# The short end of a perceiver layer: silu by tanh between gelus, a norm shared by two engines, a shorter scale chain, two output banks

## The chip, the core and the metric

The kernel runs on one core of one Trainium2 chip. The metric is the device time in microseconds. Before the change the median of three runs is 2131.52 us (2131.42 to 2131.52). Profiles name the engines PE (TensorE's products), PEld (its weight loads), DVE (VectorE), ACT (ScalarE), POOL (GpSimd) and SP (which issues most DMAs).

## The reference

One layer works on `x` (128 rows of 512) with a context of 12544 rows. Cut to what matters here:

```python
x = x + xattn(layernorm(x), ctx)             # 16 heads of 128, softmax over 12544 rows
x = x + lightning(layernorm(x))              # 16 heads of 32, silu(q), silu(k), silu(v), decay, gate, rms norm
x = x + ffn(layernorm(x))

def ffn(x):                                  # 512 -> 2048 -> 512
    h = gelu(silu(bitlinear158(x, w1, b1)))  # gelu by erf
    h = layer_norm(h, ln_g, ln_b)
    return bitlinear158(h, w2, b2)

def bitlinear158(x, w, b):
    x = x * rsqrt(mean(x * x) + 1e-5)
    scale = 127 / max(max(abs(x)), 1e-5)     # one per row
    xq = clip(round(x * scale), -128, 127) / scale
    return xq @ weight_quant(w).T + b        # weights -1, 0, 1 times their mean size
```

## The kernel before, in words

**The long part** takes the first 2040 us. Scores of the cross attention (L190) and their weighing of the context (L469) are formed on TensorE from operands split in a high and a low part. Jobs of later stages are laid beside the weighing: the weights of the feed-forward part are loaded, averaged, quantized and left in SBUF as BF16 (`w1q`, `w2q`), and `inverse` (L611) makes the reciprocals of their sizes.

**The short part** is a chain of small stages on one tile of 128 rows. `seq` keeps the instructions that it wraps in the order in which the program gives them; the rest is placed by the tile framework. Buffers of a pool are reused when the last reader is done. The stages, with their lines:

- `values` (L740) and `outs` (L761) end the cross attention, group by group. Weights for them and for the next stage come as 1 MB loads through SP's queue (helpers at L635 and L641), in the three buffers that `weight_tile` (L482) deals out in turn. Wk, Wq and Wv of the second attention are loaded during `outs(1)` to `outs(3)`, its Wo after the projections.
- `keep_warm` (L88) issues products of zeros, 128x512 in BF16, into a bank that nobody reads. They occupy TensorE where it would otherwise be idle.
- The second attention normalizes (L830 to L840), projects (`project_T`, L851; L875), forms the scores of 16 heads (`psc`, L889), multiplies by the decay (L901) and by the values (`po2`, L904: one product of 32 columns per head), gates and normalizes (L911 to L924), and projects onto `pp`, two banks of 256 columns (L930, L933).
- The feed-forward part normalizes `pp` to `xf`, finds the row's largest magnitude (L990), makes the scale `s` (`quant_scales`), raises by the constant MAGIC to round (`rounded`, L959 to L962), transposes (L968) and bounds (L973). The first product (`ph`, L1009) is taken out of PSUM with scale and bias in four quarters of 512 (L1010), ScalarE applies silu to each (L1011) and then gelu (L1013); VectorE gathers the statistics (L1014, L1024). Each quarter is then normalized in two steps, (h - mean) * g (L1030) and that times 1/deviation plus b (L1031); ScalarE squares it with a row sum (L1032), VectorE takes its largest magnitude (L1033). Row sum and maximum give the second scale, the quarters are rounded, transposed and multiplied by `w2q` into one bank `py` (L1048), and the result is scaled, added to `x2` and stored in two halves (L1064, L1065). `x2` holds attention output plus `b2` (L1001).
- 20 fillers of another kind (L1018) and 65 of `keep_warm` stand between the first product and the transposes of the second.

Of the kernel before, what the change touches and what calls it, by code (L numbers as in the profile page):

```python
# [16 lines left out]
P = 128  # L17
D = 512
# [15 lines left out]
def tile_perceiver_layer(  # L34
# [42 lines left out]
    left = const.tile([P, 24], F32, name="left")  # L77
# [531 lines left out]
    inv = const.tile([P, 2], F32, name="inv")  # L609

    def inverse():  # L611
        seq(nc.vector.tensor_scalar(m12, m12, 1.0 / (FF * D), EPS, ALU.mult, ALU.max))
        seq(nc.vector.reciprocal(inv, m12))
# [162 lines left out]
    wo[3] = by_rows(x_wo, 3)  # L776

# [16 lines left out]
    a_w = [by_cols(a_wk, 0)]  # L794
    outs(2)
    a_w.append(by_cols(a_wq, 0))
    outs(3)
    a_w.append(by_cols(a_wv, 0))
    wg1 = ctp.tile([P, NC, P], F32, tag="hi", name="wg1")
    nc.gpsimd.memset(wg1, 0.0)  # L800
    nc.sync.dma_start(out=wg1[:, :, :LHD], in_=a_wg1.rearrange("(c p) k -> p c k", p=P))
    wg2 = ctp.tile([P, D], F32, tag="hi", name="wg2")
    nc.gpsimd.memset(wg2, 0.0)
    nc.sync.dma_start(out=wg2[:LHD, :], in_=a_wg2)
    nwb = ctp.tile([P, 2, D], F32, tag="lo", name="nwb")
    nc.sync.dma_start(out=nwb[:, 0, :], in_=a_norm_w.partition_broadcast(P))
    nc.sync.dma_start(out=nwb[:, 1, :], in_=b2.partition_broadcast(P))
# [4 lines left out]
    zeros_r = work.tile([P, 512], F32R, name="zeros_r")  # L812
    nc.gpsimd.memset(zeros_r.bitcast(F32), 0.0)
    late = [keepp.tile([P, 8, 512], F32, name=f"uT{f}") for f in range(2)]
# [49 lines left out]
    seq(nc.scalar.activation(qT, project_T(a_w[1]), AF.Silu))  # L864
    seq(nc.scalar.activation(kT, project_T(a_w[0]), AF.Silu))
    a_w.append(by_rows(a_wo, 0))
# [7 lines left out]
    for cc in range(NC):  # L874
        seq(nc.tensor.matmul(pv, lhsT=xaT[:, cc, :], rhs=a_w[2][:, cc, :], start=(cc == 0), stop=(cc == NC - 1)))  # L875
# [23 lines left out]
    for r in range(4):  # L899
        sc = late[1][:, 4 + r, :].rearrange("p (e q) -> p e q", e=NC)  # L900
        seq(nc.vector.tensor_tensor(sc, pscs[r], decayed[:, r, :, :], ALU.mult))  # L901
        for e in range(NC):
            cs = slice((4 * e + r) * LHD, (4 * e + r + 1) * LHD)
            seq(nc.tensor.matmul(po2[:, cs], lhsT=sc[:, e, :], rhs=v[:, cs], start=True, stop=True))  # L904
# [22 lines left out]
    for i in range(NC):  # L927
        for half, hs in enumerate(halves):
            if i < 2:
                seq(nc.tensor.matmul(pp[half], lhsT=ogT[:, i, :], rhs=a_w[3][:, i, hs], start=False, stop=False))  # L930
    for half, hs in enumerate(halves):
        for i in (2, 3):
            seq(nc.tensor.matmul(pp[half], lhsT=ogT[:, i, :], rhs=a_w[3][:, i, hs], start=False, stop=(i == 3)))  # L933
    keep_warm(ps_w, 14)
# [3 lines left out]
    def quant_scales(am, rms):  # L938


        floor = col("floor")
        seq(nc.vector.tensor_scalar(floor, rms, EPS, None, ALU.mult))
        step_ = col("step")
        s = col("s")
        seq(nc.vector.tensor_scalar(step_, am, floor, 1.0 / 127.0, ALU.max, ALU.mult))
# [10 lines left out]
    def rounded(dst, y, s, engine):  # L956

        if engine is nc.scalar:
            seq(nc.scalar.activation(y, y, AF.Identity, scale=s, bias=magic))  # L959
        else:  # L960
            seq(nc.vector.tensor_scalar(y, y, s, MAGIC, ALU.mult, ALU.add))
        seq(nc.vector.tensor_scalar(dst, y, -MAGIC, 127.0, ALU.add, ALU.min))  # L962
# [19 lines left out]
    less = col("less")  # L982
    seq(nc.vector.tensor_scalar(less, mv1[:, 0:1], -1.0, None, ALU.mult))
    rms1 = col("rms")
    seq(nc.scalar.activation(rms1, mv1[:, 1:2], AF.Sqrt, scale=1.0 + EPS, bias=eps2))
    xf = work.tile([P, D], F32, tag="xa", name="xf")
    seq(nc.scalar.activation(xf[:, halves[1]], pp[1], AF.Identity, bias=less))
    seq(nc.vector.tensor_scalar(xf[:, halves[0]], pp[0], mv1[:, 0:1], None, ALU.subtract))
    am1 = col("am")
    seq(nc.vector.tensor_reduce(am1, xf, AX.X, ALU.max, apply_absolute_value=True))  # L990
    s1, step1 = quant_scales(am1, rms1)
# [125 lines left out]
```

## Time and profile before

| | |
|---|---|
| median of three runs | 2131.52 us |
| profiled execution | 2134.19 us, its span 2132.5 us |
| long part ends | 2040.6 us |
| loads for the projections of the second attention | Wk at 2061.8, Wq at 2065.3, Wv at 2068.7, Wo at 2079.6 us |
| first product of the feed-forward part starts | 2103.6 us |
| scale `s` of its second product ready | 2122.6 us |
| the two stores are issued | 2129.4 and 2129.8 us |
| ScalarE's table loads from 2062 us on | six, 1.28 us each |

In a line of the chain or timeline, start and length come first, then engine, line and tiles; "x8" counts instructions. A float32 product appears as two records. A line of groups gives count, busy time, mean length of one, and the idle time of the engine ahead of it with what ended it. PEclk is TensorE's granted clock as a share of full speed.

### The profile page before, as it was taken

What the parts mean: (1) busy time and instruction counts of PE and PEld (TensorE: products, weight loads), DVE (VectorE), ACT (ScalarE), POOL (GpSimd) and SP (SyncE); (2) the same over time, 40 slices, a digit from 0 to 9 for tenths busy, and PEclk for the clock granted to TensorE, in tenths of its full rate; (3) what the DMA queues carried; (4) which work ended last, traced back from release to release, by engine and by line L of the source; (5) the groups of instructions that cost most, each with busy time, mean ns of one, the idle gap of its engine ahead of it and who ended that gap; (6) DMA issues with size and microseconds to landing.
All of it is one profiled execution on the core that took longest, in us unless ns stands there. A gap on an engine that the chain in (4) does not pass through costs nothing.

```text
span 2132.5 us, 23984 instructions
## 1 busy us (share of the span) xinstructions
PE 2120.1 (99%) x9627; PEld 1748.0 (82%) x9627; DVE 1647.5 (77%) x1825; ACT 753.9 (35%) x844; POOL 26.1 (1%) x16
## 2 busy tenths in 40 slices
PE   8999999999999999999999999999999999999999
PEld 7888888888888888888888888888888888888885
DVE  6877777777777777778897888887787777777735
ACT  6221222212222122214444444444444444444424
POOL 0000000000000000000000000000010000000010
PEclk9999999999999999999999999999999999999999
DMA  5333333333333333346564555454444444444360
GB/s 195 146 138 128 148 135 142 138 128 148 135 142 138 129 148 136 141 158 216 210 235 158 178 178 178 173 199 144 145 141 147 148 148 148 148 145 139 133 209 25
DMA packets 70766, 326.22 MB, mean 153 GB/s; under 512 B 7264, under 2 KB 11616, under 8 KB 45184
## 3 DMA queue, kind: packets, MB, share of 16 engines
q1 hardware_dynamic: 70512, 324.57, 42.0%
q8 instruction: 75, 1.23, 0.2%
q14 instruction: 35, 0.29, 0.0%
q10 hardware_dynamic: 144, 0.13, 0.0%
HBM read 221.65 MB, written 103.02 MB: 152 GB/s over the span
## 4 chain that ended last, share of the span: by engine, by line
PE 98%; DMA 1%; DVE 0%; ACT 0%; issue 0%; SPq 0%; DVEq 0%; ACTq 0%
PE pu L469 50%; PE ps L190 44%; PE pw L92 1%; PE pc L740 1%; DMA kq<-in_x_wq_dram 1%; PE po L761 0%; PE pk L364 0%; PE pp L851 0%; DMA wq<-in_x_wq_dram 0%; DMA kq<-in_a_wq_dram 0%; PE pq L344 0%; PE po L904 0%; PE py L1048 0%; PE pv L875 0%; PE pw L1018 0%; PE pp L930 0%
## 5 line engine op out<-in xcount | busy, mean ns | idle before, releaser
L190 PE MATMUL ps<-kq,cth 128*128 128x512 f32 x2744 | 844.5, 389 | 0.0
L469 PE MATMUL pu<-ph,cl 128*128 128x512 f32 x1568 | 610.0, 389 | 0.0
L469 PE MATMUL pu<-pl,ch 128*128 128x512 f32 x1568 | 610.0, 389 | 0.0
L469 PE MATMUL pu<-ph,ch 128*128 128x512 f32 x1568 | 610.0, 389 | 0.0
L190 PEld LDWEIGHTS ps<-kq,cth 128*128 128x128 f32 x2744 | 515.0, 188 | 106.8
L190 PE MATMUL ps<-kq,ctl 128*128 128x512 f32 x1344 | 522.8, 389 | 0.0
L523 ACT CAST ph<-si 128x1024 fp32r<-128x1024 f32 x194 | 203.9, 1051 | 491.3 <-PE pu L469 491.2
L469 PEld LDWEIGHTS pu<-pl,ch 128*128 128x128 f32 x1568 | 294.3, 188 | 61.3
L469 PEld LDWEIGHTS pu<-ph,cl 128*128 128x128 f32 x1568 | 294.3, 188 | 61.0
L469 PEld LDWEIGHTS pu<-ph,ch 128*128 128x128 f32 x1568 | 294.3, 188 | 61.0
L219 DVE TENSOR_TENSOR so<-ps,u 128x512 f32<-128x512 f32 x294 | 202.9, 690 | 134.8 <-PE ps L190 130.4
L190 PEld LDWEIGHTS ps<-kq,ctl 128*128 128x128 f32 x1344 | 252.3, 188 | 52.5
L511 DVE TENSOR_TENSOR cl<-cr,ch 128x1024 fp32r<-128x1024 f32 x98 | 120.2, 1227 | 204.7 <-ACT ch L505 204.7
L254 ACT COPY so<-ps 128x512 f32<-128x512 f32 x98 | 57.7, 589 | 577.5 <-PE ps L190 577.5
L528 DVE TENSOR_TENSOR pl<-si,ph 128x1024 fp32r<-128x1024 f32 x194 | 242.5, 1250 | 1.0 <-ACT ph L523 1.0
L237 DVE TENSOR_TENSOR mx<-mx,so 128x1024 f32<-128x1024 f32 x190 | 232.3, 1223 | 6.7
L517 DVE TENSOR_TENSOR si<-si,mb 128x1024 f32<-128x1024 f32 x194 | 235.7, 1215 | 0.0
L536 DVE TENSOR_TENSOR lsum<-lsum,si 128x1024 f32<-128x1024 f32 x192 | 233.9, 1218 | 0.0
L518 ACT ACTIVATE si<-si 128x1024 f32<-128x1024 f32 x194 | 205.5, 1059 | 61.0 <-DVE si L517 61.0
L505 ACT CAST ch<-cr 128x1024 fp32r<-128x1024 f32 x98 | 102.3, 1044 | 0.3 <-DMA cr<-in_c_dram 0.3
L176 DVE TENSOR_TENSOR ctl<-ctr,cth 128x1792 fp32r<-128x1792 f32 x47 | 94.9, 2019 | 0.7 <-ACT cth L171 0.7
L171 ACT CAST cth<-ctr 128x1792 fp32r<-128x1792 f32 x48 | 81.7, 1703 | 37.5 <-PE ps L190 35.4
(210 smaller groups left out, 769.2 us busy)
## 6 DMA issues: line engine op xcount, KB each, us to landing
sc<-so SPq DMA_DIRECT2D x98, 1024.0 KB, 3.8
si<-sc SPq DMA_DIRECT2D x97, 1024.0 KB, 4.9
cr<-in_c_dram SPq DMA_DIRECT2D x98, 512.0 KB, 3.4
ctr<-in_cT_dram SPq DMA_DIRECT2D x48, 512.0 KB, 3.5
kq<-in_w1T_dram SPq DMA_DIRECT2D x16, 512.0 KB, 4.6
kq<-in_w2T_dram SPq DMA_DIRECT2D x16, 512.0 KB, 4.8
kq<-in_x_wv_dram SPq DMA_DIRECT2D x3, 1024.0 KB, 5.4
kq<-in_x_wo_dram SPq DMA_DIRECT2D x3, 1024.0 KB, 7.4
```

The costliest lines, as they stand in the source:

```text
L176: return lo, nc.vector.tensor_tensor(lo, raw[:, :7, :, :], hi, ALU.subtract)
L190: nc.tensor.matmul(ps, lhsT=lt[:, a, cc, :], rhs=right(f, b, part)[:, cc, :], start=(first and n == 0), stop=(n == 5), skip_group_check=True,)
L219: place(nc.vector.tensor_tensor(to, t[p], t[q], ALU.add))
L237: place(nc.vector.tensor_tensor(mx[f], mx[f], t["so"][:, j, :], ALU.max))
L469: nc.tensor.matmul(pu[b][cc], lhsT=lt[:, j, cs], rhs=rt[:, bs], start=(first and n == 0), stop=(last and n == 2))
L505: seq(nc.scalar.copy(ctx_hi[f, i], ctx_raw[f, i]))
L511: seq(nc.vector.tensor_tensor(ctx_lo[f, i], ctx_raw[f, i], ctx_hi[f, i], ALU.subtract))
L517: seq(nc.vector.tensor_tensor(exps[k], exps[k], mb[f], ALU.subtract))
L518: seq(nc.scalar.activation(exps[k], exps[k], AF.Exp))
L523: seq(nc.scalar.copy(high[k], exps[k]))
L528: seq(nc.vector.tensor_tensor(low[k], exps[k], high[k], ALU.subtract))
L536: seq(nc.vector.tensor_tensor(lsum[f], lsum[f], exps[k], ALU.add))
```

## The change

- Wq of the second attention is loaded into the upper half of the first context sum's buffer (`uT0`, free after `values(1)`), ahead of `wo[3]`; Wk, Wv and Wo follow in the three dealt buffers. The small loads and memsets stand earlier in the program.
- The `po2` products of head r of four are 128, 96, 64 and 32 columns wide: each writes also the columns of later heads, which the later products overwrite.
- The floor under a scale is a constant and no longer EPS times the row's size; the maxima are joined in pieces, the sign of `xf` is turned (and of `s`), the sums of squares are used only for `dq2`.
- The additions into `x2` follow the four L1010. Quarters 0 and 1 keep silu on ScalarE; for quarters 2 and 3, ScalarE gives tanh(h/2), VectorE (tanh + 1) * h, and gelu takes half of it. Gelus, tanhs, multiplications and statistics are interleaved in a written order.
- In the last norm, quarter 0 stays on VectorE. For quarters 1 to 3 TensorE adds identity times b and diagonal(1/deviation) times (h - mean) g in PSUM, where squares, maxima and rounding read them.
- The second rounding raises all quarters first, begins with a half quarter, and its product goes into two banks of 256 columns. Filler counts change: 14 to 13 ahead of the first rounding, 20 + 65 to 12 + 14 behind it.

```diff
+    inv = const.tile([P, 3], F32, name="inv")
+    m1_neg = inv[:, 2:3]
     def inverse():
         seq(nc.vector.tensor_scalar(m12, m12, 1.0 / (FF * D), EPS, ALU.mult, ALU.max))
-        seq(nc.vector.reciprocal(inv, m12))
+        seq(nc.vector.reciprocal(inv[:, :2], m12))
+        seq(nc.vector.tensor_scalar(m1_neg, m12[:, 0:1], -1.0, None, ALU.mult))
...
     outs(0)
     wo[3] = by_rows(x_wo, 3)
+    late = [keepp.tile([P, 8, 512], F32, name="uT0")]
+    a_w = {"q": by_cols(a_wq, 0, lambda shape: late[0][:, 4:, :])}
...
     outs(1)
     values(3)
-    a_w = [by_cols(a_wk, 0)]
+    late.append(keepp.tile([P, 8, 512], F32, name="uT1"))
+    a_w["k"] = by_cols(a_wk, 0)
     outs(2)
-    a_w.append(by_cols(a_wq, 0))
+    a_w["v"] = by_cols(a_wv, 0)
     outs(3)
-    a_w.append(by_cols(a_wv, 0))
...
-    zeros_r = work.tile([P, 512], F32R, name="zeros_r")
-    nc.gpsimd.memset(zeros_r.bitcast(F32), 0.0)
-    late = [keepp.tile([P, 8, 512], F32, name=f"uT{f}") for f in range(2)]
     keep_warm(ps_w, 8)
...
         seq(nc.vector.tensor_tensor(sc, pscs[r], decayed[:, r, :, :], ALU.mult))
         for e in range(NC):
-            cs = slice((4 * e + r) * LHD, (4 * e + r + 1) * LHD)
+            cs = slice((4 * e + r) * LHD, (4 * e + 4) * LHD)
             seq(nc.tensor.matmul(po2[:, cs], lhsT=sc[:, e, :], rhs=v[:, cs], start=True, stop=True))
...
-    keep_warm(ps_w, 14)
+    keep_warm(ps_w, 13)
     x2 = late[1][:, 4, :]
-    def quant_scales(am, rms):
-        floor = col("floor")
-        seq(nc.vector.tensor_scalar(floor, rms, EPS, None, ALU.mult))
+    def quant_scales(am, others, sign):
         step_ = col("step")
         s = col("s")
-        seq(nc.vector.tensor_scalar(step_, am, floor, 1.0 / 127.0, ALU.max, ALU.mult))
+        seq(nc.vector.tensor_scalar(step_, am, others, sign / 127.0, ALU.max, ALU.mult))
         seq(nc.vector.reciprocal(s, step_))
         return s, step_
...
-    def rounded(dst, y, s, engine):
+    def raised(t, y, s, engine):
         if engine is nc.scalar:
-            seq(nc.scalar.activation(y, y, AF.Identity, scale=s, bias=magic))
+            seq(nc.scalar.activation(t, y, AF.Identity, scale=s, bias=magic))
         else:
-            seq(nc.vector.tensor_scalar(y, y, s, MAGIC, ALU.mult, ALU.add))
-        seq(nc.vector.tensor_scalar(dst, y, -MAGIC, 127.0, ALU.add, ALU.min))
+            seq(nc.vector.tensor_scalar(t, y, s, MAGIC, ALU.mult, ALU.add))
+    def rounded(dst, t):
+        seq(nc.vector.tensor_scalar(dst, t, -MAGIC, 127.0, ALU.add, ALU.min))
...
         seq(nc.vector.bn_stats(out=st1[:, half, :], in_=pp[half]))
     mv1 = small.tile([P, 2], F32, tag="mv", name="mv1")
     seq(nc.vector.bn_aggr(out=mv1, in_=st1))
-    less = col("less")
-    seq(nc.vector.tensor_scalar(less, mv1[:, 0:1], -1.0, None, ALU.mult))
+    xf = work.tile([P, D], F32, tag="xa", name="xf")
+    am1 = small.tile([P, 2], F32, tag="am1", name="am1", bufs=1)
+    seq(nc.scalar.activation(xf[:, halves[1]], pp[1], AF.Identity, scale=-1.0, bias=mv1[:, 0:1]))
+    seq(nc.vector.tensor_scalar(xf[:, halves[0]], pp[0], -1.0, mv1[:, 0:1], ALU.mult, ALU.add))
     rms1 = col("rms")
     seq(nc.scalar.activation(rms1, mv1[:, 1:2], AF.Sqrt, scale=1.0 + EPS, bias=eps2))
-    xf = work.tile([P, D], F32, tag="xa", name="xf")
-    seq(nc.scalar.activation(xf[:, halves[1]], pp[1], AF.Identity, bias=less))
-    seq(nc.vector.tensor_scalar(xf[:, halves[0]], pp[0], mv1[:, 0:1], None, ALU.subtract))
-    am1 = col("am")
-    seq(nc.vector.tensor_reduce(am1, xf, AX.X, ALU.max, apply_absolute_value=True))
-    s1, step1 = quant_scales(am1, rms1)
+    seq(nc.vector.tensor_reduce(am1[:, 0:1], xf[:, halves[0]], AX.X, ALU.max, apply_absolute_value=True))
+    seq(nc.vector.tensor_scalar(am1[:, 0:1], am1[:, 0:1], EPS * EPS, None, ALU.max))
+    seq(nc.vector.tensor_reduce(am1[:, 1:2], xf[:, halves[1]], AX.X, ALU.max, apply_absolute_value=True))
+    s1, step1 = quant_scales(am1[:, 1:2], am1[:, 0:1], -1.0)
     xq = work.tile([P, D], BF16, tag="g1T", name="xq")
     xqT = work.tile([P, NC, P], BF16, tag="xqT", name="xqT")
-    rounded(xq[:, halves[0]], xf[:, halves[0]], s1, nc.vector)
-    rounded(xq[:, halves[1]], xf[:, halves[1]], s1, nc.scalar)
+    for hs, engine in zip(halves, (nc.vector, nc.scalar)):
+        raised(xf[:, hs], xf[:, hs], s1, engine)
+        rounded(xq[:, hs], xf[:, hs])
     ptx = [transposed_b(xq[:, hs]) for hs in halves]
     for half in range(2):
         bounded(xqT[:, 2 * half : 2 * half + 2, :], ptx[half])
-    dq1 = taken_back(step1, rms1, m12[:, 0:1])
-    for half, hs in enumerate(halves):
-        seq(nc.vector.tensor_tensor(x2[:, hs], pp[half], nwb[:, 1, hs], ALU.add))
+    dq1 = taken_back(step1, rms1, m1_neg)
     hb = late[0][:, 4:, :].rearrange("p a b -> p (a b)")
     st = small.tile([P, 4, 6], F32, tag="bn4", name="st", bufs=1)
     fss = [slice(f * 512, (f + 1) * 512) for f in range(4)]
-    for fs in fss:
+    for f, fs in enumerate(fss):
         ph = ps_m.tile([P, 512], F32, tag="m", name="ph")
         for cc in range(NC):
             nc.tensor.matmul(ph, lhsT=xqT[:, cc, :], rhs=w1q[cc // 2][:, cc % 2, fs], start=(cc == 0), stop=(cc == NC - 1))
-        nc.vector.scalar_tensor_tensor(hb[:, fs], ph, dq1, rows["b1"][:, fs], ALU.mult, ALU.add)
-        seq(nc.scalar.activation(hb[:, fs], hb[:, fs], AF.Silu))
-    for f, fs in enumerate(fss):
-        seq(nc.scalar.activation(hb[:, fs], hb[:, fs], AF.Gelu))
-        nc.vector.bn_stats(out=st[:, f, :], in_=hb[:, fs])
...
...
-    keep_warm(ps_w, 65)
+        seq(nc.vector.scalar_tensor_tensor(hb[:, fs], ph, dq1, rows["b1"][:, fs], ALU.mult, ALU.add))
+        if f < 2:
+            seq(nc.scalar.activation(hb[:, fs], hb[:, fs], AF.Silu))
+    curve = late[1][:, 6:, :]
+    def bent(f):
+        seq(nc.scalar.activation(curve[:, f - 2, :], hb[:, fss[f]], AF.Tanh, scale=0.5))
+    def gelu(f):
+        seq(nc.scalar.activation(hb[:, fss[f]], hb[:, fss[f]], AF.Gelu, scale=1.0 if f < 2 else 0.5))
+    def times(f):
+        seq(nc.vector.scalar_tensor_tensor(hb[:, fss[f]], curve[:, f - 2, :], 1.0, hb[:, fss[f]], ALU.add, ALU.mult))
+    def spread(f):
+        seq(nc.vector.bn_stats(out=st[:, f, :], in_=hb[:, fss[f]]))
+    for half, hs in enumerate(halves):
+        seq(nc.vector.tensor_tensor(x2[:, hs], pp[half], nwb[:, 1, hs], ALU.add))
+    for do, f in (
+        (gelu, 0), (bent, 2), (spread, 0), (gelu, 1), (times, 2), (bent, 3), (spread, 1), (gelu, 2), (times, 3),
+        (spread, 2), (gelu, 3), (spread, 3),
+    ):
+        do(f)
     mv = small.tile([P, 2], F32, tag="mv", name="mv")
-    nc.vector.bn_aggr(out=mv, in_=st)
-    rh = row_rsqrt(mv[:, 1:2])
+    seq(nc.vector.bn_aggr(out=mv, in_=st))
+    pn = {}
+    for f, (pool, tag) in zip((1, 2, 3), ((ps_s, "s"), (ps_m, "m"), (ps_m, "m"))):
+        pn[f] = pool.tile([P, 512], F32, tag=tag, name="pn")
+        seq(nc.tensor.matmul(pn[f], lhsT=ident, rhs=rows["lb"][:, fss[f]], start=True, stop=False))
+    keep_warm(ps_w, 12)
+    rh = col("rh")
+    seq(nc.scalar.activation(rh, mv[:, 1:2], AF.Sqrt, bias=eps_t))
+    diagonal = work.tile([P, P], F32, tag="g1T", name="diagonal")
     sm4 = small.tile([P, 4], F32, tag="sm4", name="sm4", bufs=1)
-    am4 = small.tile([P, 4], F32, tag="am4", name="am4", bufs=1)
+    am5 = small.tile([P, 5], F32, tag="am5", name="am5", bufs=1)
+    seq(nc.vector.memset(am5[:, 0:1], EPS * EPS**0.5))
     junk = late[1][:, 5, :]
     for f, fs in enumerate(fss):
-        nc.vector.scalar_tensor_tensor(hb[:, fs], hb[:, fs], mv[:, 0:1], rows["lg"][:, fs], ALU.subtract, ALU.mult)
-        nc.vector.scalar_tensor_tensor(hb[:, fs], hb[:, fs], rh, rows["lb"][:, fs], ALU.mult, ALU.add)
-        nc.scalar.activation(junk, hb[:, fs], AF.Square, accum_out=sm4[:, f : f + 1])
-        nc.vector.tensor_reduce(am4[:, f : f + 1], hb[:, fs], AX.X, ALU.max, apply_absolute_value=True)
-    sm2, am2 = col("sm"), col("am")
+        seq(nc.vector.scalar_tensor_tensor(hb[:, fs], hb[:, fs], mv[:, 0:1], rows["lg"][:, fs], ALU.subtract, ALU.mult))
+        if f == 0:
+            seq(nc.vector.reciprocal(rh, rh))
+            seq(nc.scalar.mul(diagonal, ident, rh))
+        else:
+            seq(nc.tensor.matmul(pn[f], lhsT=diagonal, rhs=hb[:, fs], start=False, stop=True))
+    seq(nc.vector.scalar_tensor_tensor(hb[:, fss[0]], hb[:, fss[0]], rh, rows["lb"][:, fss[0]], ALU.mult, ALU.add))
+    whole = {**pn, 0: hb[:, fss[0]]}
+    for f in (1, 0, 2, 3):
+        seq(nc.scalar.activation(junk, whole[f], AF.Square, accum_out=sm4[:, f : f + 1]))
+    others = col("others")
+    for f in range(4):
+        if f == 3:
+            seq(nc.vector.tensor_reduce(others, am5[:, 0:4], AX.X, ALU.max))
+        seq(nc.vector.tensor_reduce(am5[:, f + 1 : f + 2], whole[f], AX.X, ALU.max, apply_absolute_value=True))
+    keep_warm(ps_w, 14)
+    s2, step2 = quant_scales(am5[:, 4:5], others, 1.0)
+    hq = work.tile([P, FF], BF16, tag="hq", name="hq")
+    py = [ps_v.tile([P, 256], F32, tag="v", name="py") for _ in range(2)]
+    hT = [work.tile([P, NC, P], BF16, tag="hT", name="hT", bufs=2) for _ in range(4)]
+    def outward(ns, halves_):
+        for n in ns:
+            for half in halves_:
+                seq(
+                    nc.tensor.matmul(
+                        py[half], lhsT=hT[n // 4][:, n % 4, :], rhs=w2q[n // 8][:, n % 8, halves[half]],
+                        start=(n == 0), stop=(n == NF - 1),
+                    )
+                )
+    raised(hb[:, halves[0]], hb[:, halves[0]], s2, nc.vector)
+    raised(hb[:, halves[1]], hb[:, halves[1]], s2, nc.scalar)
+    for f in (1, 2, 3):
+        raised(hb[:, fss[f]], pn[f], s2, nc.scalar)
+    pts = {}
+    for half in range(2):
+        rounded(hq[:, halves[half]], hb[:, halves[half]])
+        pts[half] = transposed_b(hq[:, halves[half]])
+    bounded(hT[0][:, 0:2, :], pts[0])
+    outward((0, 1), range(2))
+    rounded(hq[:, fss[1]], hb[:, fss[1]])
+    bounded(hT[0][:, 2:4, :], pts[1])
+    pts[1] = transposed_b(hq[:, fss[1]])
+    outward((2, 3), range(2))
+    for f in (2, 3):
+        rounded(hq[:, fss[f]], hb[:, fss[f]])
+        bounded(hT[f - 1], pts[f - 1])
+        pts[f] = transposed_b(hq[:, fss[f]])
+        outward(range(4 * f - 4, 4 * f), range(2))
+    bounded(hT[3], pts[3])
+    sm2, rms2 = col("sm"), col("rms")
     seq(nc.vector.tensor_reduce(sm2, sm4, AX.X, ALU.add))
-    seq(nc.vector.tensor_reduce(am2, am4, AX.X, ALU.max))
-    rms2 = col("rms")
     seq(nc.scalar.activation(rms2, sm2, AF.Sqrt, scale=1.0 / FF, bias=eps_t))
-    s2, step2 = quant_scales(am2, rms2)
-    hq = work.tile([P, FF], BF16, tag="hq", name="hq")
-    py = ps_v.tile([P, D], F32, tag="v", name="py")
-    hT = [work.tile([P, NC, P], BF16, tag="hT", name="hT", bufs=2) for _ in range(4)]
-    def outward(f):
-        bounded(hT[f], pts[f])
-        for n in range(4 * f, 4 * f + 4):
-            seq(
-                nc.tensor.matmul(
-                    py, lhsT=hT[f][:, n % 4, :], rhs=w2q[n // 8][:, n % 8, :], start=(n == 0), stop=(n == NF - 1)
-                )
-            )
-    pts = []
-    for f, fs in enumerate(fss):
-        rounded(hq[:, fs], hb[:, fs], s2, nc.scalar if f else nc.vector)
-        pts.append(transposed_b(hq[:, fs]))
-        if f > 0:
-            outward(f - 1)
     dq2 = taken_back(step2, rms2, m12[:, 1:2])
-    outward(3)
+    outward(range(12, 16), (0,))
+    outward(range(12, 16), (1,))
     y = work.tile([P, D], F32, tag="xa", name="y")
-    for half in range(2):
-        hs = slice(half * 256, (half + 1) * 256)
-        seq(nc.vector.scalar_tensor_tensor(y[:, hs], py[:, hs], dq2, x2[:, hs], ALU.mult, ALU.add))
+    for half, hs in enumerate(halves):
+        seq(nc.vector.scalar_tensor_tensor(y[:, hs], py[half], dq2, x2[:, hs], ALU.mult, ALU.add))
         (nc.sync, nc.scalar)[half].dma_start(out=out[:, hs], in_=y[:, hs])
     keep.close()
     att.close()
```

## The prediction

> **What bounds the kernel now.** I read the page's busy times and chain first, then the chain in order of time over the last 70 us, then groups, clock and single engines there. Page:
>
> ```profile
> PE 2120.1 (99%) x9627; PEld 1748.0 (82%) x9627; DVE 1647.5 (77%) x1825; ACT 753.9 (35%) x844; POOL 26.1 (1%) x16
> PE 98%; DMA 1%; DVE 0%; ACT 0%; issue 0%; SPq 0%; DVEq 0%; ACTq 0%
> ```
>
> TensorE is the bound, but the diff touches nothing of the two products (L190, L469) that fill it until 2040.6 us. What it touches lies behind, where the 98% mislead: much of TensorE's work there is filler on zeros (`pw`). The chain in order of time (start, us, what):
>
> ```profile
> 2065.28 6.73 DMA kq<-in_a_wq_dram
> ...
> 2087.15 3.73 PE po L904 x32
> 2090.87 4.25 PE pw L92 x13
> ...
> 2107.48 2.30 PE pw L1018 x20
> 2109.82 14.19 PE pw L92 x65
> 2124.01 0.24 PE ptb L968 x4
> ```
>
> Three things are to be seen: the projections wait for the load of Wq; 13 fillers take 4.25 us, 0.327 each, where 65 take 0.218 each; and the last fillers end at 2124.01, later than the `hq` that the transposes need. The clock explains the second (stretch, length, TensorE busy, granted clock, DMA share, GB/s):
>
> ```profile
> 2083.42:2086.84 3.42, 3.41 (x40) 1.00 0.25 95
> 2086.84:2090.25 3.41, 3.41 (x32) 1.00 0.00 0
> 2090.25:2093.66 3.41, 3.41 (x12) 0.50 0.00 0
> ```
>
> The stretch at half clock follows 3.1 us of `po2` products only 32 columns wide. They come 0.115 us apart like 128-column ones, so I estimate that each streams a quarter of that. Under the other fillers (L1018, L92 x65) the true chain runs on ScalarE and VectorE (groups since 2062; count, then busy, mean ns, idle before):
>
> ```profile
> L1010 DVE SCALAR_TENSOR_TENSOR uT<-ph,dq,row_b 128x512 f32<-128x512 f32 x4 | 3.0, 748 | 0.5 <-PE ph L1009 0.4
> L1031 DVE SCALAR_TENSOR_TENSOR uT<-uT,rsr,row_lb 128x512 f32<-128x512 f32 x4 | 2.8, 746 | 0.0
> L1033 DVE TENSOR_REDUCE am<-uT 128x1 f32<-128x512 f32 x4 | 2.5, 678 | 0.0
> L1014 DVE BATCH_NORM_STATS2 st<-uT 128x6 f32<-128x512 f32 x4 | 2.5, 681 | 2.6 <-ACT uT L1013 2.6
> L1013 ACT ACTIVATE uT<-uT 128x512 f32<-128x512 f32 x4 | 2.2, 618 | 0.0
> L1013 ACT ACT_TABLE_LOAD x1 | 1.3, 1283 | 0.0
> L959 ACT ACTIVATE uT<-uT,right,s 128x512 f32<-128x512 f32 x3 | 2.2, 803 | 0.7 <-DVE s L946 0.7
> L875 PE MATMUL pv<-kq,xaT 128*128 128x512 f32 x8 | 3.6, 592 | 0.0
> ```
>
> In the timeline, successive operations of one engine start about 0.08 us before the other ends when they are independent. A result is seen by another engine 0.03 to 0.05 us later, and a matmul's 0.17 us after its stream.
>
> **The change part by part**, in times of before.
>
> *Load of Wq.* It moves ahead of `wo[3]` in SP's queue, to about 2048.2, into `uT0`, which is free once `values(1)` is done. The product (L851) then waits only for ScalarE's copy `xaT`, which ends at 2071.74, so it starts at 2071.80 and not 2072.14: **0.34 us**. Behind Wq stand `wo[3]`, two rows, Wk, Wv, Wo; the queue moves some 310 GB/s there, so one more MB delays each by 3.4 us. `wo[3]` lands near 2062 (needed 2065.3), Wk near 2072.5 (needed 2075.4), Wv near 2075.5 (needed 2079.8), all covered; Wk 3 us later still would stall TensorE by what exceeds its cover. The POOL memsets and the mask move too: `df` now stands behind four reciprocals, so `decay` is complete near 2060 and is needed at 2085.9. Nothing.
>
> *Wider `po2`.* Widths 128, 96, 64, 32 at the same 0.115 us cost nothing, as L740's 128 columns at 0.112 show. I estimate the window's streaming at 2.06 of 3.41 us, 60%, against 30% before; the window 2069.77 to 2073.18, some 59% by the same count, kept its clock. So the 13 fillers take 2.8 us and end at 2093.3. The transposes then wait for VectorE (L924, first half done near 2093.4) and the copy for L930 ends 0.9 us later: L930 starts at 2094.35 in place of 2095.80. Beyond the 0.34 that is **1.1 us**. If the clock still falls it is nothing.
>
> *First scale.* `less` and `floor` go, the maximum is taken in halves (410 + 150 + 410 ns against 690 + 140): `s` comes 0.05 us sooner. The reciprocal sign and `m1_neg` are free, the latter within the long loop.
>
> *First product's way out.* The two additions into `x2` (0.61 us) move behind the four L1010. The first now starts when `ph` is done, 2104.52 for 2104.80; the second ends at 2106.12. Two silu instead of four follow, so the Gelu table is loaded from 2106.80 to 2108.08, where before it began at 2108.95: 2.15 us. Two tanh (618 ns, as L1013; built without a table load between) and two multiplications (748) come in. VectorE is now what orders it: after gelu 0 at 2108.72 it runs statistics, multiplication, statistics, multiplication, starting 0.60 to 0.67 apart, to 2111.36; the last gelu ends at 2112.00, its statistics at 2112.71, the aggregate at 2113.00 (was 2113.69). ScalarE's root is seen at 2113.61 (was 2114.04).
>
> *Norm shared.* VectorE keeps four L1030 and one L1031 instead of four; three are replaced by an identity and a diagonal product each, 0.86 us apiece (two records of 0.43, as L875). Identity products and 12 fillers end by 2112.4 under the gelus. The four L1030 and the reciprocal run to 2115.87, L1031 to 2116.53; diagonal products are done at 2115.63, 2116.50, 2117.35. Squares take 720 ns with their accumulator: 2116.38, then the one on the SBUF quarter 2117.28, 2118.03, 2118.78. In the built program each maximum over a PSUM bank waits for the square of that bank. The Trainium skill (PSUM — Partial Sum Buffer, Terms) says why: two engines on one bank at once collide, reads against reads included. The row is before's L1033, which read the same SBUF quarter while L1032 squared it. By the row `s` would be 0.3 us sooner; I take the rule, as the waits are in the program. So the third maximum starts at 2118.05, the fourth at 2118.85, and `s`, with 0.1 us for doubled waits, is ready at 2120.05 (was 2122.57): 2.5 us.
>
> *Rounding and output.* Roots and row sums leave the scale's chain. From `s` to the second `y` before: 7.18 us. Now the first transposes wait for a half (350 + 290 ns), not for fillers that overran by 0.45; ScalarE's 600 + 3 x 711 ns, then the last transposes, 0.42 us of bounding and eight 256-column products of 0.11 follow, and the first `y` runs beside the second bank's products. Followed through, that is 6.55 us: 0.65 less. The late `dq2` is ready within 0.05 us of the first bank. With 0.05 and 2.5, this is **3.15** after rounding.
>
> Sum: 0.34 + 1.1 + 3.15 = 4.6. The profiled execution took 2134.19 (span 2132.5) and would take 2129.6; the runs' median 2131.52 lies 2.67 below it, and I carry the difference over: **2126.9**.
>
> *What may take back a part.* Between the 12 fillers and the first diagonal product TensorE is idle for 2.2 us (2112.4 to 2114.6); before, fillers stood there. The row above says that 30% streaming in a 3.41 us window, without any idling, cost the clock in the next. If one window holds all of the gap, it streams 35%. The skill (TensorE: Matmul & The Clock Gate, Why this matters for your kernels) says that idle gaps must not exceed some 3 us. By the rule 2126.9 stands. By the row two diagonal products take 0.86 more each and the next 14 fillers, which otherwise end 0.4 us before the transposes, end 1.0 after their due time: 2127.9. The threshold is between 30 and 59%, the window must lie just so and the gap be as long as I work out; narrowly I take no loss. Both ends stay in the range.
>
> **The rivals.** (1) *Half clock for one window*, 2127.9: for it, 35% is near 30%; before's low stage and its end (2131.21, twelve times 3.413 later) put a window at 2110.73 to 2114.14, where the gap would fall; against it, the rule. (2) *The wider products don't save the clock*: 2128.0 with, 2129.0 together with (1). Against it the 59% window. (3) *Slower than before*: the clock stays at half from the diagonal products to the end. Two products, 14 fillers and all output work gain 9.1 us of TensorE time, 8.2 of it on the chain: 2135.1. It decides from about the fourth low window on (three cost 4.2, under the 4.6 gained). Against it, a TensorE kept busy at half clock got its clock back at 2093.66. (4) *More is gained*: PSUM reads on ScalarE shorter than SBUF ones (L880's 597 against L1011's 630) and fewer waits than I count: 2125.8.
>
> **How the numbers follow.** Main case 0.50 (own range 2126.1 to 2127.7), (1) 0.33, (2) 0.06, (3) 0.05, (4) 0.06. Low 2125.7 and high 2128.9 leave out (3), half of (2) and little of the tails. About 0.2%, 4.3 us, is what a measurement of this kernel can tell from no change: the bound is 2127.26. The main case passes it by 0.36: three quarters of its chance, 0.39, with 0.06 of (4) and 0.05 of (1), are faster: 0.50. Slower by over 0.2% is only the worse part of (3): 0.04. The rest, 0.46, is within.
>
> **What would show it.** L930's counterpart 1.4 us sooner with clock 1.00 ahead of it; the Gelu table load 2.1 us sooner against the chain; `s` 2.5 us sooner after the attention's last product; no filler ahead of the last transposes in the chain. Clock 0.50 behind the gap, with 14 fillers of 0.22 us each reaching into the transposes, shows (1). Wrong would be the sum if a load is waited for, or if quarters read from PSUM cost ScalarE or VectorE over a quarter more than from SBUF (each quarter more: about 1 us).

## The result and the profile after

The changed kernel takes 2128.80 us in the median of 22 runs (2127.46 to 2129.93); the kernel before, beside it, takes 2131.66 us in the median of 22 (2130.45 to 2134.92). The ratio, worked out over the runs and not from the two medians, is 0.9984, with a 95% interval from 0.9977 to 0.9991. The gain is real, but smaller than the 0.2% that I called the limit, so this counts as "within 0.2%". The prediction was 2126.9 us with a range of 2125.7 to 2128.9: the time lies 1.9 us above the forecast, just inside the range.

The profiled execution took 2127.83 us (span 2126.1) where that of before took 2134.19 (span 2132.5). These two differ by 6.4 us, more than twice as much as the medians. Why one pair of executions says so much more than 44 runs is what had to be found out. The page after, busy times and shares of the chain:

```profile
PE 2112.7 (99%) x9591; PEld 1745.2 (82%) x9595; DVE 1646.7 (77%) x1827; ACT 754.2 (35%) x846; POOL 25.7 (1%) x15
PE 98%; DVE 1%; DMA 1%; ACT 0%; SPq 0%; issue 0%; DVEq 0%; ACTq 0%
```

As before, these shares describe the long part. The end of the kernel shows in the chain in order of time (start, us, what):

```profile
2070.17 7.41 PE pp L853 x64
...
2085.20 3.51 PE po L906 x32
...
2092.64 1.99 PE pp L932 x8
...
2103.83 1.28 ACT L1025
...
2115.01 0.70 DVE am L1071
...
2117.72 0.30 PE ptb L974 x2
...
2122.11 0.28 DVE dq L956
...
2122.49 0.48 DVE y L1117
```

No load and no filler (`pw`) is left in this stretch of the chain: between the products stand VectorE and ScalarE, down to `dq2`, for which the first half of `y` waits. The long part's last stage and the short part are best read as distances, since two executions do not reach the end of the level products (`outs`) at the same time: 2068.70 us before, 2067.07 after, though the diff does not touch what fills most of that time. From there on:

| distance, us (from the two traces) | before | after | gained | predicted |
|---|---|---|---|---|
| end of `outs` to the first projection | 3.44 | 3.10 | 0.34 | 0.34 |
| first projection to output projection (L930, now L932) | 23.66 | 22.47 | 1.19 | 1.1 |
| end of output projection to first scale `s` | 2.63 | 2.64 | -0.01 | 0.05 |
| same start, to the Gelu table load | 9.42 | 7.45 | 1.97 | 2.15 |
| same start, to the aggregate's end | 14.16 | 13.57 | 0.59 | 0.69 |
| same start, to the second scale `s` | 23.04 | 20.56 | 2.48 | 2.5 |
| second `s` to the end of the second half of `y` | 7.18 | 6.43 | 0.75 | 0.65 |
| sum (rows 1, 2, 6, 7) | | | 4.76 | 4.6 |

Between these two executions nearly every step is as forecast. The other 1.6 us of their difference lie before the end of `outs`. So the question was not what the change does to the chain, but why the median keeps only 2.9 of 4.8 us.

The prediction named one place that might take something back, the idle time ahead of the diagonal products. It is there, as long as forecast (timeline of TensorE after; in brackets the idle time before it and what ended it):

```profile
2106.64 2.75 PE L92 MATMUL pw<-zeros 128*128 128x512 bf16 x12
2111.61 2.81 PE L1062 MATMUL pn<-uT,diagonal 128*128 128x512 f32 x6 [2.22 <-DVE uT L1057]
```

In this execution it cost nothing: six records in 2.81 us are products at full clock, as in gap_filled below, where TensorE does not stand idle ahead of them. But of the 22 runs of after, nine have a mean granted clock of 1.000 (median 2127.84 us) and thirteen one of 0.999 (median 2129.15). One stretch of 3.41 us at half clock is 3.41 x 0.5 / 2126 = 0.0008 of the mean, so 0.999 stands for one such stretch and 0.998 for two. The kernel before varies likewise: of 62 runs measured in the first set of experiments, 31 are at 1.000 (median 2131.61), 25 at 0.999 (2132.86), 6 at 0.998 (2134.27).

### The profile page after: what moved, and what is told of

It reads as the page before. It is cut to its first block, busy times and chain, and to the rows that moved or that the text cites. A ratio compares the mean times of both kernels' runs of the same rounds, so it can differ in the third digit from the quotient of the medians.

```text
span 2126.1 us, 23916 instructions
## 1 busy us (share of the span) xinstructions
PE 2112.7 (99%) x9591; PEld 1745.2 (82%) x9595; DVE 1646.7 (77%) x1827; ACT 754.2 (35%) x846; POOL 25.7 (1%) x15
## 4 chain that ended last, share of the span: by engine, by line
PE 98%; DVE 1%; DMA 1%; ACT 0%; SPq 0%; issue 0%; DVEq 0%; ACTq 0%
PE pu L469 50%; PE ps L190 44%; PE pc L742 1%; PE po L763 1%; PE pk L364 1%; DMA kq<-in_x_wq_dram 1%; PE pp L853 0%; PE pq L344 0%; PE po L906 0%; PE pv L876 0%; SPq L300 0%; DVE uT L1057 0%; DVE st L1031 0%; PE pp L932 0%; ACT kq L409 0%
## 5 line engine op out<-in xcount | busy, mean ns | idle before, releaser
L190 PE MATMUL ps<-kq,cth 128*128 128x512 f32 x2744 | 844.5, 389 | 0.0
L190 PEld LDWEIGHTS ps<-kq,cth 128*128 128x128 f32 x2744 | 515.2, 188 | 106.6
L190 PE MATMUL ps<-kq,ctl 128*128 128x512 f32 x1344 | 522.8, 389 | 0.0
L190 PEld LDWEIGHTS ps<-kq,ctl 128*128 128x128 f32 x1344 | 252.3, 188 | 52.4
```

What stands on the lines that cost most here:

```text
L190: nc.tensor.matmul(ps, lhsT=lt[:, a, cc, :], rhs=right(f, b, part)[:, cc, :], start=(first and n == 0), stop=(n == 5), skip_group_check=True,)
```

## The experiments

**First set: who pays for the clock, and how often.** Two kernels change only the number of fillers ahead of the diagonal products, two exchange the width of the `po2` products.

```
gap_filled (after):          gap_wide (after):
-    keep_warm(ps_w, 12)     -    keep_warm(ps_w, 12)
+    keep_warm(ps_w, 22)     +    keep_warm(ps_w, 2)

po2_narrow (gap_filled):
-            cs = slice((4 * e + r) * LHD, (4 * e + 4) * LHD)
+            cs = slice((4 * e + r) * LHD, (4 * e + r + 1) * LHD)
before_po2_wide (before): the reverse
```

> The changed kernel with 22 fillers in place of 12 ahead of the diagonal products, so that TensorE's idle gap of 2.2 us there shrinks to about 0.1 us. Theory A (the gap costs the clock in some executions, about 1 us each): the granted clock is 1.0 in every run, the median falls by 0.8 to 1.3 us to about 2127.7, and the spread between runs shrinks. Theory B (the runs of the changed kernel differ for reasons at the kernel's start, and the gap costs nothing): the median stays at 2128.8 within 0.3 us and the runs spread as before.

> The changed kernel with 2 fillers in place of 12, so that the gap is 4.4 us, longer than one 3.41 us window. Theory A: every execution loses the clock for one window; the two or three diagonal products and the 14 fillers run at half clock for a part, the last transposes wait for fillers, and the median is 2129.1 to 2129.8 with clock 0.999 in all runs. Theory B: the clock doesn't matter for the time, the median stays at 2128.8 within 0.3 us.

> The changed kernel with the gap filled (22 fillers) and the products into po2 again 32 columns wide. If the prediction's step is right: a window at half clock around the 13 fillers ahead of the attention's transposes, and 1.1 us more than with wide products (2128.8 where that gives 2127.7). If the width doesn't matter for the clock: the same time within 0.2 us.

> The kernel before with the po2 products alone made 128, 96, 64 and 32 columns wide. If the step is right: clock 1.0 through the fillers at 2091 us, the product L930 starts 1.1 to 1.4 us sooner after the projections, and the time falls by 1.1 us (ratio 0.9995). Rival (the half clock there stands only in the profiled execution, most runs don't have it): no difference in the median, although the profile shows a clock of 1.0.

| kernel | median us (runs) | ratio to before, interval | runs by granted clock |
|---|---|---|---|
| before, same set | 2132.08 (62) | | 31 at 1.000, 25 at 0.999, 6 at 0.998 |
| gap_filled | 2128.28 (21) | 0.9981 [0.9975, 0.9988] | all at 1.000 |
| gap_wide | 2129.95 (21) | 0.9988 [0.9982, 0.9995] | 10 at 0.999, 11 at 0.998 |
| po2_narrow | 2128.67 (18) | 0.9985 [0.9977, 0.9992] | 7 at 1.000, 8 at 0.999, 3 at 0.998 |
| before_po2_wide | 2131.58 (13) | 0.9998 [0.9989, 1.0006] | all at 1.000 |

The intervals of the times overlap; the granted clocks do not leave room for doubt. With the gap filled no run loses the clock, with the gap made 4.4 us long every run does, with 2.2 us thirteen of 22. The timeline of gap_filled shows the gap closed:

```profile
2107.76 4.91 PE L92 MATMUL pw<-zeros 128*128 128x512 bf16 x22
2112.73 2.81 PE L1062 MATMUL pn<-uT,diagonal 128*128 128x512 f32 x6
```

In its times gap_filled meets neither theory: the median lies 0.5 us under that of after, between the 0.8 to 1.3 of A and the 0.3 of B, and the runs spread as widely (2.48 us against 2.47). The two were measured in different sets, though: each against the before of its own set, gap_filled gains 3.8 us and after 2.9. That the nine runs of after at clock 1.000 have 2127.84, less than gap_filled, points to the same shift between the sets, since from the end of `outs` on the two traces are alike to 0.02 us.

gap_wide shows how the clock is lost. Stretches of TensorE alone (stretch, length, TensorE busy, granted clock, DMA share, GB/s):

```profile
2107.40:2110.80 3.40, 0.00 (x0) 1.00 0.00 0
2110.80:2114.20 3.40, 2.64 (x3) 0.50 0.00 0
2114.20:2117.64 3.44, 3.44 (x6) 0.50 0.00 0
2117.64:2121.00 3.36, 3.08 (x18) 1.00 0.00 0
```

Idle for one stretch, half clock in the next two: the first of these, busy for 2.64 of 3.40 us, did not bring the full clock back. The clock comes back by itself, but the chain in order of time has lost 2.6 us in the diagonal products, and the fillers behind them become late for the transposes:

```profile
2111.56 5.46 PE pn L1062 x6
2117.02 3.39 PE pw L92 x14
2120.41 0.13 PE ptb L974 x2
```

The six records take 5.46 us in place of 2.81, fillers are in the chain again, as they were in before, and the end of `y` comes 29.54 us after the output projection, 2.5 later than in gap_filled. The median, 2129.95, is a little above the forecast of 2129.1 to 2129.8, which reckoned with one stretch for every run; 11 of 21 lost two.

For `po2` the two traces agree with the prediction: first projection to output projection takes 23.71 us in po2_narrow and 22.48 in gap_filled. In po2_narrow the 13 fillers behind the narrow products show the half clock, in the chain in order of time:

```profile
2085.82 3.49 PE po L906 x32
2089.31 4.49 PE pw L92 x13
```

That is 0.345 us for each of 13, against 0.218 at full clock. before_po2_wide has 22.45 us in the same stretch (its 13 fillers take 2.97 us) and no run below 1.000. But the median of before_po2_wide is only 0.5 us below that of before, with an interval that holds 1, and po2_narrow's is only 0.4 above gap_filled's. The traces say 1.2 us, the medians half of that or less, and the clocks say why: half of the runs of before, and 7 of 18 of po2_narrow, never paid. The 1.2 us are a price of some executions.

Why some? The Trainium skill (TensorE: Matmul & The Clock Gate, the part on the HAM clock gate) says that activity is judged in windows of 3413 ns which run freely and do not start with the kernel. The runs agree: stretches at half clock are 3.41 us long here (before, and norm_on_vector below; in gap_wide two in a row), and the same code loses the clock in one execution and not in the next. That a window must hold enough of the weak stretch fits with it; where the windows lay in runs that were not profiled is not shown.

**Second set: what each part is worth once the clock is kept.** All of these start from gap_filled, so that their difference to it is not a matter of windows. Distances are again from the traces: from the end of the output projection to `s`, and to the end of `y`; gap_filled has 20.58 and 27.00 us. Each kernel was also timed, in two further sets (median of before there 2132.37 in 59 runs and 2131.97 in 49, against 2132.08 beside gap_filled). The times of gap_filled alone spread over 2.5 us, so below half a microsecond the distances tell.

*The norm on VectorE alone.*

```
-        seq(nc.tensor.matmul(pn[f], lhsT=ident, rhs=rows["lb"][:, fss[f]], start=True, stop=False))
...
-            seq(nc.tensor.matmul(pn[f], lhsT=diagonal, rhs=hb[:, fs], start=False, stop=True))
...
+    for fs in fss:
+        seq(nc.vector.scalar_tensor_tensor(hb[:, fs], hb[:, fs], rh, rows["lb"][:, fs], ALU.mult, ALU.add))
...
-    keep_warm(ps_w, 22)
+    keep_warm(ps_w, 34)
...
-    keep_warm(ps_w, 14)
+    keep_warm(ps_w, 26)
```

> The kernel after with the weak stretch of TensorE filled (as in gap_filled), and the last norm on VectorE alone again: no identity and diagonal products, all four scale-and-bias instructions on VectorE, squares, maxima and raising from SBUF. The whole reference is computed. Theory A (sharing the norm is worth what the sum says): VectorE is the engine on the path from the aggregate to `s`, so three more instructions of 0.60 to 0.67 us, less 0.2 for the square that the maxima wait for in gap_filled, make `s` 1.6 us later (from 20.6 us after the last product of the attention part to 22.2) and the time 1.6 us longer than gap_filled (2128.3 to 2129.9). Theory B (the norm is not on the path, since the maxima wait for ScalarE's squares on the same banks): `s` under 0.5 us later and the time within 0.5 us of gap_filled.

Measured: `s` at 22.09 us, 1.51 later (Theory A). The time was 2130.86 us (12 runs, ratio 0.9992 [0.9984, 1.0001]), 2.6 over gap_filled, not 1.6, and the distance to the end of `y` was 30.15, 3.15 longer. Seven of 12 runs have a clock of 0.999. My fillers had run out 1.9 us ahead of the transposes, and the next window paid. Timeline of TensorE, then stretches as above:

```profile
2104.03 13.33 PE L92 MATMUL pw<-zeros 128*128 128x512 bf16 x60
2119.26 0.49 PE L974 MATMUL ptb<-identb,hq 128*128 128x128 bf16 x4 [1.91 <-DVE hq L968]
```

```profile
2113.85:2117.26 3.41, 3.41 (x17) 1.00 0.00 0
2117.26:2120.68 3.42, 1.33 (x14) 1.00 0.00 0
2120.68:2124.09 3.41, 3.41 (x23) 0.50 0.00 0
2124.09:2126.50 2.41, 1.84 (x17) 1.00 0.00 0
```

TensorE was busy for 1.33 of 3.42 us (39%), and the whole next 3.41 us ran at half clock, under the products of the output. That this was the cause, and not the norm, was put to the test with eight fillers more.

```
norm_filled (norm_on_vector):
-    keep_warm(ps_w, 26)
+    keep_warm(ps_w, 34)
```

> norm_on_vector with 8 fillers more behind the maxima (34 in place of 26), so that TensorE has work until the transposes of the last quantized rows. The whole reference is computed. Theory A (of the 3.15 us that norm_on_vector was longer between the attention part's last product and y's end, 1.5 were the norm and the rest a stretch at half clock, opened by the 1.9 us that TensorE stood idle ahead of the transposes): clock 1.00 in every run, 28.5 us in that stretch where norm_on_vector had 30.15 and gap_filled 27.0, and the time 1.5 us over gap_filled. Theory B (it was something else in the norm on VectorE): 30 us or more, as before.

Measured: 2129.44 us (20 runs, ratio 0.9988 [0.9981, 0.9995]), clock 1.000 in all 20; `s` at 22.09, end of `y` at 28.60. Eight products of zeros gave back 1.55 us of the distance. The shared norm is worth 1.5 us at `s` and 1.6 at the end.

*Silu on all four quarters.*

```
-        if f < 2:
-            seq(nc.scalar.activation(hb[:, fs], hb[:, fs], AF.Silu))
+        seq(nc.scalar.activation(hb[:, fs], hb[:, fs], AF.Silu))
...
-        (gelu, 0), (bent, 2), (spread, 0), (gelu, 1), (times, 2), (bent, 3), (spread, 1), (gelu, 2), (times, 3),
-        (spread, 2), (gelu, 3), (spread, 3),
+        (gelu, 0), (spread, 0), (gelu, 1), (spread, 1), (gelu, 2), (spread, 2), (gelu, 3), (spread, 3),
```

> The kernel after with the weak stretch of TensorE filled, and silu as such on all four quarters: no tanh, no multiplication, the gelus unscaled. The whole reference is computed. Theory A (the tanh form is worth little once its own work is counted): the Gelu table is loaded 1.5 us later than in gap_filled (two more silu ahead of it), but two tanh of 0.52 us and two multiplications of 0.60 us behind it go, the four gelus follow each other at 0.52 us, and the last gelu ends at 12.6 us after the last product of the attention part, as it does in gap_filled: aggregate and time 0 to 0.2 us later than gap_filled. Theory B (the earlier table load passes through): aggregate 0.6 us later or more, as far as 1.5, and the time with it.

Measured: 2128.62 us (20 runs, all at 1.000; ratio 0.9983 [0.9976, 0.9990]). The aggregate ends at 14.06 us, 0.48 later, and the end of `y` is 0.48 later. Neither theory has it right: nearer to B, which asked for 0.6. I had watched the last gelu, which ends only 0.26 us later, but VectorE had become the limit. Its timeline:

```profile
2108.90 2.47 DVE L1030 BATCH_NORM_STATS2 st<-uT 128x6 f32<-128x512 f32 x4 [1.98 <-ACT uT L1024]
```

Four statistics take 0.62 us each from the first gelu on, while the gelus come 0.52 apart. VectorE idles for 1.98 us until the late table load is over, and must then do them all. With tanh, statistics and multiplications begin 1.87 us sooner, as the table is loaded 1.87 us sooner, and use that time; two multiplications more take most of it back. So the head start of 1.87 us is worth 0.48.

*One bank for the output.*

```
-    outward(range(12, 16), (0,))
-    outward(range(12, 16), (1,))
+    outward(range(12, 16), range(2))
```

(and `py` one tile of 512 columns, each product 512 wide)

> The kernel after with the weak stretch of TensorE filled, and the last products into one bank of 512 columns, both halves of y after the last product. The whole reference is computed. Theory A (two banks let the first half of y run beside the last four products, but dq2 holds it back): y's second half ends 0.3 us later than in gap_filled, counted from `s`. Theory B (dq2 alone sets the start of y): no difference, under 0.1 us. Theory C (the whole of one y instruction is hidden by two banks): 0.45 us later.

Measured: from `s` to the end of `y` 6.72 us against 6.42 in gap_filled, 0.30 longer: Theory A. 2128.87 us (20 runs, ratio 0.9985 [0.9978, 0.9992]).

*The row's scale earlier.*

```
-    bounded(hT[3], pts[3])
-    sm2, rms2 = col("sm"), col("rms")
-    seq(nc.vector.tensor_reduce(sm2, sm4, AX.X, ALU.add))
-    seq(nc.scalar.activation(rms2, sm2, AF.Sqrt, scale=1.0 / FF, bias=eps_t))
     dq2 = taken_back(step2, rms2, m12[:, 1:2])
+    bounded(hT[3], pts[3])
```

(sum behind the maxima, root behind the last raising)

> The kernel after with the weak stretch of TensorE filled, and the row's scale dq2 worked out early: the sum of the squares behind the maxima, the square root behind ScalarE's last raising, reciprocal and dq2 ahead of the last lower bound. The whole reference is computed. Theory A (dq2 is what the first half of y waits for): both halves of y end about 0.15 us sooner than in gap_filled, counted from `s` (6.27 in place of 6.42), `s` no later. Theory B (the two instructions ahead of the last lower bound on VectorE, 0.4 us, delay it and with it the last products): 0.2 to 0.4 us later. Neither is told by the times, which scatter by 1 us: the stretch in the trace tells.

Measured: 6.36 us in place of 6.42, so 0.06 sooner where 0.15 was expected; the start of `y` comes 0.11 sooner. `y` now starts when its products are done (timeline of VectorE):

```profile
2122.19 0.92 DVE L1117 SCALAR_TENSOR_TENSOR y<-py,dq,uT 128x256 f32<-128x256 f32 x2 [0.89 <-PE py L1084]
```

The time is 2127.96 us (13 runs, ratio 0.9979 [0.9971, 0.9987]), the lowest median of all, but not told from gap_filled's.

*The floor from the root mean square.*

```
-    s2, step2 = quant_scales(am5[:, 4:5], others, 1.0)
+    seq(nc.vector.tensor_reduce(sm2, sm4, AX.X, ALU.add))
+    seq(nc.vector.tensor_reduce(am2, am5[:, 1:5], AX.X, ALU.max))
+    seq(nc.scalar.activation(rms2, sm2, AF.Sqrt, scale=1.0 / FF, bias=eps_t))
+    seq(nc.vector.tensor_scalar(floor2, rms2, EPS, None, ALU.mult))
+    s2, step2 = quant_scales(am2, floor2, 1.0)
```

(and 16 fillers in place of 14 behind the maxima)

> The kernel after with the weak stretch of TensorE filled, and the second scale's floor taken from the row's root mean square again, as in the kernel before: sum, maximum of the maxima, square root on ScalarE and floor stand between the last maximum and `s`. The whole reference is computed. Theory A (the constant floor takes the way over ScalarE off the path): `s` 0.6 us later (0.29 for the root, 0.2 for its two handovers and the floor, 0.1 for the rest), and y's end 0.4 us later, since dq2 is then early. Theory B (the root runs beside the last maximum): `s` within 0.15 us of gap_filled.

Measured: `s` at 21.09 us, 0.51 later, the end of `y` 0.45 later (Theory A by its size: 0.6 and 0.4 expected). 2128.55 us (20 runs, ratio 0.9983 [0.9976, 0.9990]).

*Wq late again.*

```
-    a_w = {"q": by_cols(a_wq, 0, lambda shape: late[0][:, 4:, :])}
+    a_w = {}
...
-    a_w["v"] = by_cols(a_wv, 0)
+    a_w["q"] = by_cols(a_wq, 0)
```

(and Wv after `outs(3)`, Wo after the k projection)

> The kernel after with the weak stretch of TensorE filled, and Wq loaded after Wk, into the buffers that are dealt round, as in the kernel before (Wv behind it, Wo after the k projection). The whole reference is computed. Theory A (the late Wq was what the first projection waited for): the first projection starts 0.3 us later after the last product of the level part, 3.4 us in place of 3.1, and the time is 0.3 us longer. Theory B (the 0.33 us between the two profiled executions was chance): no difference, under 0.05 us, in that stretch.

Measured: the end of `outs` to the first projection takes 3.10 us, as in gap_filled (3.10): Theory B. The load was issued as late as in before, 3.42 us ahead of the end of `outs` in both, and still nothing waits for it. The list of loads gives the reason (KB each, us to landing), first before, then before_po2_wide, then q_late:

```profile
kq<-in_a_wq_dram SPq DMA_DIRECT2D x1, 1024.0 KB, 6.7
```

```profile
kq<-in_a_wq_dram SPq DMA_DIRECT2D x1, 1024.0 KB, 6.5
```

```profile
kq<-in_a_wq_dram SPq DMA_DIRECT2D x1, 1024.0 KB, 5.4
```

The same megabyte was 5.4 us under way in q_late and 6.7 in before. At 6.7 the projection waits 0.34 us, at 6.5 0.14 (3.24 us in that stretch), at 5.4 nothing, with 1.1 us to spare. Whether q_late's other neighbours in the queue (two small loads and `nwb` had gone earlier) made it faster is not told apart from chance; its other loads were fast in that execution too. The time was 2128.32 us (16 runs, ratio 0.9980 [0.9972, 0.9988]), that of gap_filled.

## Why the prediction was right and wrong

**The chain.** The Gelu table load, `s`, the wider products and the output were within 0.2 us of their forecasts each, and their sum, 4.76 us by trace against 4.6, was right. (The "3.15 after rounding" is a slip: the terms named there, 0.65, 0.05 and 2.5, make 3.20. The sum stays 4.6, and the trace shows 3.22.) The parts undone one by one from gap_filled show the same: tanh 0.48, shared norm 1.60, constant floor 0.45, two banks 0.30, together 2.83 of the 3.22 us between before and gap_filled behind the output projection. What remains, 0.4, is about the size of the overrun of the 65 fillers (0.45) that the prediction counted among the rounding's gains; that was not tried alone, and parts undone one at a time need not add up. The first scale's 0.05 did not come (-0.01). The maxima on PSUM banks do wait for ScalarE's squares, as the prediction chose to count, and `s` came where that choice put it; what would happen without the wait no run here shows. The third maximum waits for 0.25 us (timeline of VectorE after):

```profile
2115.01 0.69 DVE L1071 TENSOR_REDUCE am<-pn 128x1 f32<-128x512 f32 x1 [0.25 <-ACT uT L1066]
```

**The step that failed: "I carry the difference over".** I had worked out the sum against one profiled execution of 2134.19 us, which had its stretch at half clock behind `po2`, and subtracted it whole from a median of 2131.52. The experiments show two things about that:

- *The 1.1 us of `po2` was in the profiled execution, but not in the median.* Runs of before at clock 1.000 have a median of 2131.61, and before_po2_wide, which always keeps the clock, has 2131.58. By its size the 2131.52 that I subtracted from was already the time of executions that did not pay (the clocks of those three runs are not on record). By that, 0.34 + 3.15 = 3.5 us were to be had, from 2131.61 to 2128.1. gap_filled, at 2128.28 in the same set, is there to 0.2 us; the load of Wq, whose 0.34 also depends on the execution, may be the rest, which is not shown.
- *The gap does cost, in 13 of 22 runs.* "Narrowly I take no loss" was the wrong choice as a yes or no: it is a share. Runs of after that lose the clock are 1.3 us longer than those that keep it (the forecast of rival 1 was 1.0 more). Filling the gap takes 0.5 off the median, or 0.9 if each is set against the before of its own set; 13 of 22 runs at 1.3 us each would be 0.8 on average, by my estimate.

The two nearly cancel. In the 62 runs of before 37 stretches were lost (0.60 for each run), in the 22 of after 13 (0.59): what the wider products saved, the new gap lost again. In the mean of the runs the change gains 3.4 us (2132.10 to 2128.70), close to the 3.57 of the table without its second row.

The 2.67 us by which the profiled execution stood above the median should have been the warning: if 1.2 of it was the clock stretch, it could not be gained a second time. The remainder of such differences lies ahead of the first product of the scores (L190), at 37.7 to 40.2 us: in the 13 profiled executions of this study the end of `outs` lies between 2066.34 us (q_late) and 2068.80 (one_bank), but in all of them 2028.6 us after that product. Of the first 50 us TensorE is busy for 46.39 in q_late and 43.50 in one_bank; there it waits for the loads of the first weights, and the flight of those varies as well (7.4 and 8.8 us for Wq's quarters of the cross attention in these two). Waiting is not all of it. po2_narrow is as busy as q_late (46.34), and its `outs` ends 1.34 us later: its first 32 products of L344 take 5.76 us, where q_late's take 4.13 and the next 32 take 3.74 in both. I take this for half clock at the start, as the first nine fillers also take 0.40 to 0.45 us each in every trace; the clock that the profile records reads 1.00 there, so this is not shown.

**The rivals.** Rival 1 was the nearest, in mechanism and, at 2127.9, in time, but it expected the window at one fixed place. Rival 2, that wider products don't save the clock, fell: no run of gap_filled or before_po2_wide lost it. Rival 3 fell: the clock came back after one window or two in each of the four traces that lost it. Of rival 4 one part was seen, squares from PSUM in 0.60 us against 0.63 from SBUF; it did not shorten the whole.

**The range and chances.** The time is inside the range by 0.1 us, at its upper end: it is held because the range reached to rival 1 and half of rival 2, and lies 1.1 us above the main case's own range. With so little to spare that is in part luck. "Faster" had been given 0.50 and "within 0.2%" 0.46, and the second came.

## What to carry to other kernels

A profile shows one execution. Before a cost seen in it is subtracted from a median of runs, ask whether the runs have it: the mean granted clock of each run told here that half of them did not. Where TensorE stood idle for 1.9 us or more, or ran products of 32 columns for 3.5 us, some executions paid for it and others did not. Costs of this kind are shares: a kernel that closes all such places keeps the clock in every run (34 of 34 in gap_filled and before_po2_wide) and gained 0.5 to 0.9 us in the median. And moving a table load or any other start forward gains only what the next engine in the chain can use: 1.87 us of head start became 0.48, since VectorE's statistics, not ScalarE, set the end.

## What was unexpected in the hardware

- An idle gap well under 3 us can cost the clock. With 1.91 us of idling (norm_on_vector) 7 of 12 runs lost it, with 2.2 us (after) 13 of 22, with 4.4 us (gap_wide) 21 of 21, and with the same places filled 0 of 20 and 0 of 21. The rule that the prediction went by, gaps up to some 3 us, is too generous here: a window busy for 39% was followed by one at half clock.
- A TensorE that is never idle can lose it too. Products 32 columns wide, back to back, cost it in 11 of 18 runs of po2_narrow; with 128, 96, 64 and 32 columns in 0 of 21 of gap_filled.
- One load of 1 MB (Wq), issued 3.42 us ahead of the end of `outs` each time, took 6.7 us to land in before, 6.5 in before_po2_wide, which has the same loads, and 5.4 in q_late, where other loads had gone ahead of it.
